# A graph layer on one core: more rows through ACT's DMA queue, and the aggregation with the gathered rows as the stationary side

## The chip, the core and the metric

The kernel runs on one core of one Trainium2 chip. A core has five engines that run side by side, each with its own instruction stream, in order: TensorE (PE; its weight loads are listed as PEld), VectorE (DVE), ScalarE (ACT), GpSimd (POOL) and SyncE (SP). They wait for each other on semaphores. SP, ACT and POOL can also issue DMAs; on SP and ACT these are short instructions of the engine's own queue (listed as SPq and ACTq), on POOL a gather is an instruction of about a microsecond. The metric is the device time of one execution in microseconds; less is better. The time before is a median of three runs.

## What is computed

A layer of a graph network over 12,500 nodes with 128 features and 200,000 edges, sorted by destination node:

```python
h = relu(layernorm(x))
Qv, Ku = h @ W_Q.T, h @ W_K.T
score = einsum('md,md->m', Qv[dst], Ku[src]) / sqrt(128) * exp(-edge_weight)
# of each destination's edges keep the 16 best scores, softmax over them -> alpha
agg = segment_sum(alpha[:, None] * (h[src] @ W_msg.T), dst)
out = x + relu(h @ W_self.T + agg)
```

The sum over a node's edges is linear, so the kernel sums the rows `h[src]` with the softmax's weights first and multiplies the sum by `W_msg` afterwards. The division by the softmax's denominator is a factor for each node and may come before or after that product.

## The kernel before

**Preparation.** The normalized rows `h` are written to a table in HBM (`h_tab`). Edge data are turned so that 128 edges, a chunk, lie on the 128 partitions. Fourteen chunks make a group; there are 112 groups. A group's edges reach the nodes that begin in it; one more chunk, the first of the next group, is looked at with it, so 15 chunks a group.

**Rows.** Each edge needs its source node's row of 512 bytes. Most come by POOL's indirect DMA (L183), one instruction for a chunk of 128 rows, into a buffer `hs` that holds a group; there are eight. `let_go` copies the chunk's indices on DVE (L219) and issues its gathers, two chunks at a time. Of some groups, chunk 13 comes through SP's queue and chunk 12 through ACT's instead, one row a DMA (L803), at a fixed rate: `SP_ROWS = 36` and `ACT_ROWS = 24` rows a pass. The table `slow`, made from these rates, tells which chunks these are. Before a row can be asked for, its number must be in a register of the issuing engine: `rows_named` loads up to 16 at once (L791), `rows_asked` issues so many DMAs.

**The main loop.** Its order is written out by hand (`manual_schedule`), one pass a group, and the stages of several groups are interleaved in it. In pass `i`:

- for group `i + 1`, `far_of` (PE L602, ACT L604, four parts) and `to_edges` (ACT L609) make a matrix that tells which edge belongs to which node; `edges_turned`, `away` (PE L625, ACT L627, three parts) and `places` (ACT L631) make two smaller ones, `po` for an edge's slot at its node and `ow` for the node within a window of 40 nodes that the chunk can reach (`WN = 40`, moved by `STEP = 8` nodes from chunk to chunk);
- for group `i`, `q_to_edges` (PE L642, four parts) brings each edge its node's query, and `scores` (DVE L653) multiplies it with the row;
- for group `i - 1`, `slots_by_node` (PE L667, L669) lays the scores out by node and slot, and `node_by_slots` turns them;
- for group `i - 2`, `best` (DVE L683 and on) finds the 16 best, `kept_to_edges` (PE L712) and `on_edges` (DVE) bring the result back to the edges, `exps` (ACT L729) takes exponentials;
- for group `i - 3`, `weights` (DVE L734) writes the weights `alz` by edge and node, and `sums` (PE L744, two halves of 7 and 8 chunks) adds up weighted rows by node. `alz` has a stretch of zeros around each chunk's 40 nodes, so that the 128 columns that are loaded as the stationary side cover all nodes of the group; the rows are the moving side. `sums_out` (ACT L749) divides by the denominator;
- for group `i - 4`, `sums_turned` (PE L752) and `sums_turned_out` (ACT L756) turn the sums; `products` (PE L759, L760) adds `h @ W_self.T` and the sums times `W_msg.T`; for group `i - 5`, `output` (DVE L764) and `store`.

The order on ACT around the change is, in one pass: `far` 0, the copies L756 and L592, `far` 1, three rows, `far` 2, the exponential of `best`, a copy, `far` 3, `to_edges`, seven rows, two copies, `away` 0, `away` 1, five rows, `away` 2, `sums_out`, `exps`, `places`, the loads of the next rows' numbers, nine rows. On PE the first half of `sums` stands ahead of `away` 0, the second half between `away` 1 and `away` 2. In `more`, `let_go` is called for group `i + 4` (chunks 4 to 13) and, at the end of the pass, for group `i + 5` (chunks 0 to 3); a buffer of `hs` is free when the `sums` of the group that had it are done.

Of the kernel before, what the change touches and what calls it, by code (L numbers as in the profile page):

```python
# [10 lines left out]
F32 = mybir.dt.float32  # L11
# [10 lines left out]
SP_ROWS = 36  # L22
ACT_ROWS = 24
PSUM = bass.MemoryType.PSUM

P = 128
# [9 lines left out]
GC = 14  # L36
NJ = GC + 1
# [44 lines left out]
def gnn_layer(  # L82
# [63 lines left out]

    alz = [const.tile([P, NJ * (WW + STEP)], F32, name=f"alz{i}") for i in range(2)]
    sl1 = [const.tile([P, NJ, KM + 1], F32, name=f"sl1{i}") for i in range(2)]
# [30 lines left out]
    def gather(g, j0, j1, index, table=h_tab):  # L179
        if j0 == 0:  # L180
            T[g]["hs"] = rows_pool.tile([P, GC, D], F32, name="hs", bufs=8)
        for j in range(j0, j1):
            nc.gpsimd.indirect_dma_start(  # L183
                out=T[g]["hs"][:, j, :], out_offset=None, in_=table[0:N, :],
                in_offset=bass.IndirectOffsetOnAxis(ap=index(j), axis=0))
# [104 lines left out]
    with tc.tile_pool(name="edges", bufs=1) as ep, ExitStack() as stage:  # L290
# [53 lines left out]

        jj, eq = (alz[0][0:32, NJ * KM * k:NJ * KM * (k + 1)].rearrange("p (j k) -> p j k", k=KM) for k in range(2))
        nc.gpsimd.iota(jj, pattern=[[1, NJ], [0, KM]], base=0, channel_multiplier=0,
# [9 lines left out]
        load_rows(ew_r, ew)  # L356
        nc.gpsimd.memset(alz[1], 0.0)
        nc.vector.memset(ones, 1.0)
# [42 lines left out]
        for j in range(NJ):  # L401
            nc.vector.memset(w0[:, j:j + 1], float(lead(j)))
        nc.vector.memset(alz[0], 0.0)
        for k in range(2):
# [138 lines left out]
    with tc.tile_pool(name="win", bufs=2) as win:  # L543
# [187 lines left out]
        def weights(g):  # L731
            n, kept = chunks[g], T[g]["kept"]
            nc.vector.tensor_tensor(kept[:, 0:n], T[g]["up"][:, 0:n], kept[:, 0:n], op=OP.mult)
            nc.vector.tensor_tensor(alz[g % 2].rearrange("e (j w) -> e j w", w=WW + STEP)[:, 0:n, 0:WN],  # L734
                                    T[g]["ow"][:, 0:n, :], bc(kept[:, 0:n], WN), op=OP.mult)


        def sums(g, part, at=None):
            n = chunks[g]
            if part == 0:  # L740
                T[g]["pa"] = et[:, 384:384 + P] if at is None else at
            half = n // 2
            for j in range(half) if part == 0 else range(half, n):
                nc.tensor.matmul(T[g]["pa"], lhsT=alz[g % 2][:, WW * j + PRE:WW * j + PRE + P],  # L744
                                 rhs=rows_of(g, j), start=(j == 0), stop=(j == n - 1))

        def sums_out(g):
            T[g]["agn"] = win.tile([P, D], F32, name="agn")
            nc.scalar.activation(T[g]["agn"], T[g]["pa"], AF.Copy, scale=T[g]["rden"])  # L749

        def sums_turned(g):
            nc.tensor.transpose(so[:, 2 * P:3 * P], T[g]["agn"], ident)  # L752

        def sums_turned_out(g):
            T[g]["aggT"] = win.tile([P, P], F32, name="aggT")
            nc.scalar.copy(T[g]["aggT"], so[:, 2 * P:3 * P])  # L756

        def products(g):
            nc.tensor.matmul(so[:, 3 * P:4 * P], lhsT=T[g]["hT"], rhs=wselfT, start=True, stop=False)  # L759
            nc.tensor.matmul(so[:, 3 * P:4 * P], lhsT=T[g]["aggT"], rhs=wmsgT, start=False, stop=True)  # L760

# [57 lines left out]
        for i in range(-3, G - 1):  # L819
# [18 lines left out]
            def more(k):  # L838

                if i in (-1, 0, 1):  # L840
                    g = i + 6
                else:
                    g, k = (i + 4, k + 2) if k < 5 else (i + 5, k - 5)
                    if g < 8:
                        return
                if i >= -1 and g < G:
                    let_go(g, k)
# [5 lines left out]
            more(0)  # L853
            at(i - 4, sums_turned)
            at(i + 1, far_of, 0)
            at(i - 4, sums_turned_out)
            at(i + 1, q_out)
            at(i, q_to_edges, 1)
            at(i + 1, far_of, 1)
            rows_asked("ACT", ACT_ROWS // 8)  # L860
            raw(0)
            for b in range(3):
                at(i - 1, slots_by_node, b)
            at(i + 1, far_of, 2)
            more(1)
            at(i - 2, best)
# [10 lines left out]
            at(i + 1, to_edges)  # L877
            rows_asked("ACT", ACT_ROWS * 5 // 16)
            at(i + 2, h_turned_out)
# [41 lines left out]
        def turned(g):  # L921
            sums_turned(g)
            sums_turned_out(g)

        def begun(g):
            sums(g, 0, bank("a", 1)[:, 0:P])

# [255 lines left out]
```

## Time and profile before

| | |
|---|---|
| median of three runs | 3100.45 us (3090.87 to 3109.37) |
| the profiled execution | 3112.28 us, span 3110.5 us |
| busy PE, PEld | 2052.1, 1692.2 us (66%, 54%) |
| busy DVE, ACT | 1264.1, 1041.8 us (41%, 33%) |
| busy POOL | 1457.7 us (47%) |
| mean granted clock of PE | 0.741 |

A row of a timeline reads: start and length in us from the span's start, engine, line, operation, what it writes and reads, how many like it in a row, and in brackets how long the engine was idle before and what ended that. `remote` there means that the semaphore's update can't be put down to an instruction, `issue` that nothing in the profile explains the wait. In a group's row, the numbers behind the bar are busy time and the mean length in ns, then idle time before it. In a table of windows, each row has the window, its length, then busy time and count of PE, PEld, DVE, ACT and POOL, then PE's granted clock, the share of the DMA engines and GB/s. An f32 matmul is recorded as two matmuls and two weight loads.

### The profile page before, as it was taken

The page shows a single profiled execution, that of the slowest core. Times are in us where ns is not written, and L with a number is a line of the kernel's source. Part 1 is how long each engine was busy: PE and PEld are TensorE (multiplying, and loading weights), DVE is VectorE, ACT ScalarE, POOL GpSimd, SP SyncE. Part 2 cuts the span into 40 slices and gives each one's busy share as a digit, 9 for nine tenths or more (in the row PEclk, how much of TensorE's full clock was granted, in tenths as well). Part 3 has the DMA queues.
Part 4 walks back from the last instruction along what each step waited for, and adds up shares of the span by engine and source line. Part 5 has one row for each costly group of instructions (what it writes and reads, how often), then busy time and mean ns, then how long its engine had stood idle before and what let it go on. Part 6 is the DMA issues. An engine that isn't in the chain of part 4 may idle for free. (4 is left out here: it accounts for less than half of the span.)

```text
span 3110.5 us, 55712 instructions
## 1 busy us (share of the span) xinstructions
PE 2052.1 (66%) x13800; PEld 1692.2 (54%) x13801; DVE 1264.1 (41%) x7016; ACT 1041.8 (33%) x2190; POOL 1457.7 (47%) x1529
## 2 busy tenths in 40 slices
PE   0256666666677667676676666776676666667667
PEld 0145555555555555555565555555565555555556
DVE  4453334433344334443433333434434433344346
ACT  4443323333333233333333333333333332333333
POOL 6524444444444444444444445444445444444440
PEclk9867777767777776777777777767767777777779
DMA  8201111111111111111111111111111111111110
GB/s 218 62 24 43 50 43 42 43 39 44 43 42 44 42 44 42 43 42 42 44 44 42 42 43 44 42 40 43 44 44 44 43 42 42 44 43 41 42 40 12
DMA packets 113004, 144.38 MB, mean 46 GB/s; under 512 B 36775, under 2 KB 86567, under 8 KB 111904
## 3 DMA queue, kind: packets, MB, share of 16 engines
q0 software_dynamic: 48512, 99.39, 12.6%
q1 hardware_dynamic: 59038, 40.04, 4.7%
q8 instruction: 109, 1.79, 0.2%
q14 instruction: 225, 1.84, 0.2%
q10 hardware_dynamic: 5120, 1.32, 0.2%
HBM read 126.79 MB, written 14.40 MB: 45 GB/s over the span
## 5 line engine op out<-in xcount | busy, mean ns | idle before, releaser
L183 POOL DMA_INDIRECT hs<-h_tab,ix x1456 | 1394.9, 958 | 1540.6 <-PE e L744 605.4
L744 PEld LDWEIGHTS e<-hs,alz 128*128 128x128 f32 x3142 | 612.1, 296 | 291.9 <-issue 280.5
L744 PE MATMUL e<-hs,alz 128*128 128x128 f32 x3142 | 668.9, 393 | 0.0
L642 PE MATMUL q<-q,to_e 128*128 128x128 f32 x3348 | 589.9, 324 | 44.9 <-issue 42.9
L642 PEld LDWEIGHTS q<-q,to_e 128*128 128x128 f32 x3348 | 545.9, 234 | 121.5 <-issue 87.5
L604 ACT ACTIVATE far<-a,minus 128x512 bf16<-128x512 f32 (+1 forms) x447 | 294.6, 659 | 891.9 <-issue 344.2
L653 DVE SCALAR_TENSOR_TENSOR prod<-hs,dec_all,q 128x128 f32<-128x128 f32 x1623 | 470.2, 342 | 133.6 <-remote 60.1
L602 PE MATMUL a<-rel,ident 112*128 112x512 bf16 (+1 forms) x447 | 211.0, 472 | 426.0 <-issue 264.4
L627 ACT ACTIVATE aw<-a 128x400 bf16<-128x400 f32 x336 | 169.4, 504 | 836.7 <-PE a L625 450.4
L683 DVE TENSOR_SCALAR ell<-slots,e 128x40 f32<-128x40 f32 x112 | 27.9, 249 | 933.6 <-remote 390.2
L625 PE MATMUL a<-minus_at,pdT 32*128 32x400 bf16 x336 | 146.6, 436 | 376.1 <-ACT aw L627 245.4
L669 PE MATMUL e<-opo,sl 128*41 128x40 f32 x3348 | 236.9, 252 | 34.0 <-issue 33.9
L669 PEld LDWEIGHTS e<-opo,sl 128*41 128x41 f32 x3348 | 215.7, 168 | 43.5 <-issue 31.3
L667 PEld LDWEIGHTS <-zrow 1*41 1x41 bf16 x112 | 11.3, 101 | 412.3 <-issue 412.2
L609 ACT ACTIVATE to_e<-far 128x1920 f32<-128x1920 bf16 x112 | 201.3, 1797 | 3.4
L764 DVE SCALAR_TENSOR_TENSOR o<-s,x_t 128x128 f32<-128x128 f32 x112 | 32.6, 291 | 403.2 <-ACT up L729 350.1
L625 PEld LDWEIGHTS <-pdT 32*128 32x128 bf16 x336 | 31.4, 94 | 190.5 <-ACT pdT L618 122.9
L631 ACT ACTIVATE opo<-aw 128x1200 f32<-128x1200 bf16 x112 | 134.7, 1202 | 0.1
L653 DVE DVE_READ_ACCUMULATOR prod<-hs,dec_all,q 128x1 f32 x1623 | 132.0, 81 | 0.0
L219 DVE COPY ix<-idx_all 128x2 int32<-128x2 int32 (+1 forms) x747 | 126.1, 183 | 0.0
L712 PEld LDWEIGHTS <-to_e 128*128 128x128 bf16 x1674 | 68.0, 111 | 94.4 <-DVE km L695 88.0
L712 PE MATMUL x<-km,to_e 128*128 128x43 bf16 x1674 | 76.7, 202 | 58.4 <-DVE km L695 58.3
(197 smaller groups left out, 1868.0 us busy)
## 6 DMA issues: line engine op xcount, KB each, us to landing
lateSP<-h_tab SPq DMA_DIRECT2D x3968, 0.5 KB
lateACT<-h_tab ACTq DMA_DIRECT2D x2560, 0.5 KB
hs<-h_tab,ix POOLq DMA_INDIRECT x1456
h_r<-h_tab SPq DMA_DIRECT2D x112, 64.0 KB
x_t<-in_x_dram SPq DMA_DIRECT2D x108, 64.0 KB
out_dram<-o SPq DMA_DIRECT2D x108, 64.0 KB
xg<-in_x_dram SPq DMA_DIRECT2D x2, 1400.0 KB
h_tab<-xg SPq DMA_DIRECT2D x2, 1400.0 KB
```

Source lines behind the costliest of these rows:

```text
L183: nc.gpsimd.indirect_dma_start(out=T[g]["hs"][:, j, :], out_offset=None, in_=table[0:N, :], in_offset=bass.IndirectOffsetOnAxis(ap=index(j ...
L602: nc.tensor.matmul(pr[:, 0:n1 - n0], lhsT=upper(ident[0:RR, g:g + 1]).to_broadcast([RR, P]), rhs=rel[:, n0:n1], start=True, stop=True)
L604: nc.scalar.activation(T[g]["far"][:, n0:n1], pr[:, 0:n1 - n0], AF.Square, bias=minus)
L609: nc.scalar.activation(T[g]["to_e"][:, 0:n], T[g]["far"][:, 0:n], AF.Relu, bias=1.0, scale=-1.0)
L625: nc.tensor.matmul(pr[:, 0:400], lhsT=T[g]["pdT"], rhs=minus_at.rearrange("k w j s -> k (w j s)")[:, n0:n1], start=True, stop=True)
L627: nc.scalar.activation(T[g]["aw"][:, n0:n1], pr[:, 0:400], AF.Square)
L631: nc.scalar.activation(T[g]["opo"].rearrange("e w j s -> e (w j s)"), T[g]["aw"], AF.Relu, bias=1.0, scale=-1.0)
L642: nc.tensor.matmul(pq[:, (j - j0) * P:(j - j0 + 1) * P], lhsT=T[g]["to_e"][:, j * P:(j + 1) * P], rhs=T[g]["q"], start=True, stop=True)
L653: nc.vector.scalar_tensor_tensor(prod, rows_of(g, j), dec_all[:, c:c + 1], T[g]["pq", b][:, (j % 4) * P:(j % 4 + 1) * P], op0=OP.mult, op1 ...
L669: nc.tensor.matmul(et[0:KM + 1, STEP * j:STEP * j + WN], lhsT=sl1[g % 2][:, j, :], rhs=T[g]["ow"][:, j, :], start=False, stop=(j == n - 1))
L712: nc.tensor.matmul(px[:, j, 0:KM + 3], lhsT=upper(T[g]["to_e"][:, j * P:(j + 1) * P]), rhs=upper(T[g]["km"]), start=True, stop=True)
L744: nc.tensor.matmul(T[g]["pa"], lhsT=alz[g % 2][:, WW * j + PRE:WW * j + PRE + P], rhs=rows_of(g, j), start=(j == 0), stop=(j == n - 1))
```

## The change

It has three parts.

1. `ACT_ROWS` goes from 24 to 40, and the rows are asked for in more places of the pass: three behind each of `far` 0, 1 and 2, seven behind `to_edges`, three behind each `away`, and 15 behind `places`.
2. In `sums` the sides are exchanged: the gathered rows (128 columns) are loaded as the stationary side, and the chunk's weights, now without zeros around them, are the moving side with 40 columns. Each chunk adds into its window of 40 columns of a PSUM area that a matmul of zeros clears first. The sums come out turned, so the transposition goes: `sums_out` copies them, `messages` multiplies by `W_msg.T`, `messages_out` divides by the denominator, and `products` adds that with the identity as the stationary side.
3. `alz` shrinks from 2400 to 600 columns for each of its two buffers, their two memsets go, and `hs` gets a ninth buffer: `more` lets go one group further ahead.

```diff
-ACT_ROWS = 24
+ACT_ROWS = 40
-    alz = [const.tile([P, NJ * (WW + STEP)], F32, name=f"alz{i}") for i in range(2)]
+    alz = [const.tile([P, NJ, WN], F32, name=f"alz{i}") for i in range(2)]
-            T[g]["hs"] = rows_pool.tile([P, GC, D], F32, name="hs", bufs=8)
+            T[g]["hs"] = rows_pool.tile([P, GC, D], F32, name="hs", bufs=9)
-        nc.gpsimd.memset(alz[1], 0.0)
-        nc.vector.memset(alz[0], 0.0)
...
-            nc.vector.tensor_tensor(alz[g % 2].rearrange("e (j w) -> e j w", w=WW + STEP)[:, 0:n, 0:WN],
+            nc.vector.tensor_tensor(alz[g % 2][:, 0:n, :],
                                     T[g]["ow"][:, 0:n, :], bc(kept[:, 0:n], WN), op=OP.mult)
         def sums(g, part, at=None):
             n = chunks[g]
             if part == 0:
-                T[g]["pa"] = et[:, 384:384 + P] if at is None else at
+                T[g]["pa"] = et[:, 304:304 + WW] if at is None else at
+                nc.tensor.matmul(T[g]["pa"], lhsT=zrow[:, 0:P], rhs=zrow, start=True, stop=False)
             half = n // 2
             for j in range(half) if part == 0 else range(half, n):
-                nc.tensor.matmul(T[g]["pa"], lhsT=alz[g % 2][:, WW * j + PRE:WW * j + PRE + P],
-                                 rhs=rows_of(g, j), start=(j == 0), stop=(j == n - 1))
+                nc.tensor.matmul(T[g]["pa"][:, STEP * j:STEP * j + WN], lhsT=rows_of(g, j),
+                                 rhs=alz[g % 2][:, j, :], start=False, stop=(j == n - 1))
         def sums_out(g):
+            T[g]["aggT"] = win.tile([P, P], F32, name="aggT")
+            nc.scalar.copy(T[g]["aggT"], T[g]["pa"][:, PRE:PRE + P])
+
+        def messages(g):
+            nc.tensor.matmul(so[:, 2 * P:3 * P], lhsT=T[g]["aggT"], rhs=wmsgT, start=True, stop=True)
+
+        def messages_out(g):
             T[g]["agn"] = win.tile([P, D], F32, name="agn")
-            nc.scalar.activation(T[g]["agn"], T[g]["pa"], AF.Copy, scale=T[g]["rden"])
-
-        def sums_turned(g):
-            nc.tensor.transpose(so[:, 2 * P:3 * P], T[g]["agn"], ident)
-
-        def sums_turned_out(g):
-            T[g]["aggT"] = win.tile([P, P], F32, name="aggT")
-            nc.scalar.copy(T[g]["aggT"], so[:, 2 * P:3 * P])
+            nc.scalar.activation(T[g]["agn"], so[:, 2 * P:3 * P], AF.Copy, scale=T[g]["rden"])
         def products(g):
             nc.tensor.matmul(so[:, 3 * P:4 * P], lhsT=T[g]["hT"], rhs=wselfT, start=True, stop=False)
-            nc.tensor.matmul(so[:, 3 * P:4 * P], lhsT=T[g]["aggT"], rhs=wmsgT, start=False, stop=True)
+            nc.tensor.matmul(so[:, 3 * P:4 * P], lhsT=ident, rhs=T[g]["agn"], start=False, stop=True)
...
-                if i in (-1, 0, 1):
+                if i in (-1, 0, 1, 2):
                     g = i + 6
                 else:
-                    g, k = (i + 4, k + 2) if k < 5 else (i + 5, k - 5)
-                    if g < 8:
+                    g, k = (i + 5, k + 2) if k < 5 else (i + 6, k - 5)
+                    if g < 9:
                         return
...
-            at(i - 4, sums_turned)
+            at(i - 4, messages)
             at(i + 1, far_of, 0)
-            at(i - 4, sums_turned_out)
+            rows_asked("ACT", 3)
+            at(i - 4, messages_out)
             at(i + 1, far_of, 1)
-            rows_asked("ACT", ACT_ROWS // 8)
+            rows_asked("ACT", 3)
...
             at(i + 1, far_of, 2)
+            rows_asked("ACT", 3)
...
             at(i + 1, to_edges)
-            rows_asked("ACT", ACT_ROWS * 5 // 16)
+            act_names = rows_named("ACT", i + 1)
+            rows_asked("ACT", 7)
...
             at(i + 1, away, 0)
+            rows_asked("ACT", 3)
...
             at(i + 1, away, 1)
-            rows_asked("ACT")
+            rows_asked("ACT", 3)
             at(i - 3, sums, 1)
...
             at(i + 1, away, 2)
+            rows_asked("ACT", 3)
             at(i - 3, sums_out)
...
             at(i + 1, places)
-            for _ in rows_named("ACT", i + 1):
+            for _ in act_names:
                 pass
-            rows_asked("ACT", ACT_ROWS * 3 // 8)
+            rows_asked("ACT", ACT_ROWS - 25)
```

`rows_named` is a generator, so the loads still happen where it is run through, behind `places`.

More of the change, by code (lines that the diff above doesn't have):

```diff
@@ L343, in gnn_layer @@
                        allow_small_or_imprecise_dtypes=True)
-        jj, eq = (alz[0][0:32, NJ * KM * k:NJ * KM * (k + 1)].rearrange("p (j k) -> p j k", k=KM) for k in range(2))
+        jj, eq = (ep.tile([32, NJ, KM], F32, name=f"jk{k}") for k in range(2))
         nc.gpsimd.iota(jj, pattern=[[1, NJ], [0, KM]], base=0, channel_multiplier=0,
@@ L921, in turned @@
         def turned(g):
-            sums_turned(g)
-            sums_turned_out(g)
+            messages(g)
+            messages_out(g)
         def begun(g):
-            sums(g, 0, bank("a", 1)[:, 0:P])
+            sums(g, 0, bank("a", 1)[:, 0:WW])
         def all_slots(g):
```

## The prediction

> **What bounds the kernel now.** I read the page first, then one pass of the main loop in the timeline, engine by engine, then a pass near the end in which POOL has nothing left to gather, and last the busy times of four whole passes.
>
> ```profile
> span 3110.5 us, 55712 instructions
> ...
> L183 POOL DMA_INDIRECT hs<-h_tab,ix x1456 | 1394.9, 958 | 1540.6 <-PE e L744 605.4
> ...
> L744 PE MATMUL e<-hs,alz 128*128 128x128 f32 x3142 | 668.9, 393 | 0.0
> ...
> lateACT<-h_tab ACTq DMA_DIRECT2D x2560, 0.5 KB
> ```
>
> No engine on the page is near full, so a chain of waits sets the pass. I take one from the start of the long ACT operation `places` (L631) at 1505.94 to the next at 1533.37: 27.43 us. POOL's gathers come in two batches. Left out between the first and the second row are six like them, between the third and the fourth four, all 1.25 us apart (0.94 and a gap of 0.30):
>
> ```profile
> 1504.56 0.95 POOL L183 DMA_INDIRECT hs<-h_tab,ix  x1 [7.72 <-PE e L744]
> ...
> 1513.60 0.94 POOL L183 DMA_INDIRECT hs<-h_tab,ix  x1 [0.30 <-issue]
> 1518.66 0.94 POOL L183 DMA_INDIRECT hs<-h_tab,ix  x1 [4.11 <-DVE prod L653]
> ...
> 1524.90 0.94 POOL L183 DMA_INDIRECT hs<-h_tab,ix  x1 [0.30 <-issue]
> 1531.98 0.95 POOL L183 DMA_INDIRECT hs<-h_tab,ix  x1 [6.13 <-PE e L744]
> ```
>
> The same pass on ACT, PE and DVE (rows of the engines' timelines, ACT first):
>
> ```profile
> 1505.19 0.51 ACT L627 ACTIVATE aw<-a 128x400 bf16<-128x400 f32 x1 [3.65 <-PE a L625]
> 1505.59 0.36 ACT L749 ACTIVATE agn<-e,rden 128x128 f32<-128x128 f32 x1
> ...
> 1505.94 1.20 ACT L631 ACTIVATE opo<-aw 128x1200 f32<-128x1200 bf16 x1
> 1507.77 3.27 ACTq L803 DMA_DIRECT2D lateACT<-h_tab  x9
> 1511.09 0.69 ACT L604 ACTIVATE far<-a,minus 128x512 bf16<-128x512 f32 x1 [3.94 <-issue]
> 1511.67 0.26 ACT L756 COPY aggT<-s 128x128 f32<-128x128 f32 x1
> ...
> 1512.30 0.82 ACTq L803 DMA_DIRECT2D lateACT<-h_tab  x3
> ...
> 1518.97 1.80 ACT L609 ACTIVATE to_e<-far 128x1920 f32<-128x1920 bf16 x1
> 1519.03 2.04 ACTq L803 DMA_DIRECT2D lateACT<-h_tab  x7
> 1521.12 0.27 ACT L585 COPY hT<-s 128x128 f32<-128x128 f32 x1 [0.35 <-PE a L615]
> ...
> 1527.38 0.50 ACT L627 ACTIVATE aw<-a 128x400 bf16<-128x400 f32 x1 [5.68 <-remote]
> ...
> 1533.37 1.20 ACT L631 ACTIVATE opo<-aw 128x1200 f32<-128x1200 bf16 x1
> ...
> 1511.83 0.38 PE L602 MATMUL a<-rel,ident 112*128 112x512 bf16 x1 [3.53 <-ACT far L604]
> ...
> 1512.30 2.32 PE L669 MATMUL e<-opo,sl 128*41 128x40 f32 x30
> ...
> 1522.56 0.34 PE L625 MATMUL a<-minus_at,pdT 32*128 32x400 bf16 x1
> ...
> 1527.94 0.49 PE L625 MATMUL a<-minus_at,pdT 32*128 32x400 bf16 x1 [4.17 <-ACT aw L627]
> 1528.36 3.78 PE L744 MATMUL e<-hs,alz 128*128 128x128 f32 x16
> ...
> 1516.26 0.25 DVE L683 TENSOR_SCALAR ell<-slots,e 128x40 f32<-128x40 f32 x1 [8.64 <-PE a L602]
> ```
>
> Two waits look odd. `best` (DVE L683) needs the slots' matmuls (L669), whose records end at 1514.62, but starts at 1516.26: 1.72 after the first batch ended (1514.54). ACT's first `away` (L627) needs a matmul that ends at 1522.90, but starts at 1527.38: 1.54 after the second batch ended (1525.84). Where nothing is gathered, both waits are gone:
>
> ```profile
> 3033.53 1.48 PE L669 MATMUL e<-opo,sl 128*41 128x40 f32 x30
> 3035.05 0.25 DVE L683 TENSOR_SCALAR ell<-slots,e 128x40 f32<-128x40 f32 x1 [6.05 <-PE e L669]
> ...
> 3040.84 0.34 PE L625 MATMUL a<-minus_at,pdT 32*128 32x400 bf16 x1 [0.41 <-ACT pdT L618]
> ...
> 3041.22 0.50 ACT L627 ACTIVATE aw<-a 128x400 bf16<-128x400 f32 x1 [0.43 <-PE a L625]
> ```
>
> There `best` starts 0.04 after the slots and `away` 0.04 after its matmul. So while a batch is in flight, word from PE comes late, whatever the cause. The loop is then: the second half of `sums` ends and frees a rows buffer; eight gathers (1504.56 to 1514.54, 9.98); 1.72 to `best`; 2.40 to the next gather; six gathers (7.18); 1.54 to `away`; 0.98 to the second `sums`; 3.62 until POOL starts again (1531.98). Together 27.42. Whole passes with 14, 13, 12 and no gathers agree; the column before the clock is POOL (its counts take in a neighbour's gather):
>
> ```profile
> 1505.94:1533.37 27.43, 18.35 (x126) 15.33 (x125) 10.67 (x60) 8.71 (x20) 13.53 (x15) 0.75 0.16 43
> 1990.40:2016.69 26.29, 19.21 (x125) 15.70 (x124) 10.44 (x60) 8.70 (x20) 12.66 (x14) 0.69 0.17 42
> 2126.02:2148.84 22.82, 16.39 (x129) 13.38 (x128) 10.54 (x59) 8.60 (x20) 11.18 (x13) 0.84 0.18 45
> 3027.60:3045.30 17.70, 14.06 (x125) 11.96 (x125) 9.95 (x53) 8.67 (x20) 0.00 (x0) 0.90 0.03 10
> ```
>
> A second chain runs beside the first batch: last `away`, `places`, number loads, nine row issues, `far` (1511.09), PE L602 (1511.83), slots until 1514.62. It has 1516.26 - 1514.62 = 1.64 us to spare. PE idles 3.53 in it, but that idle time costs nothing as long as the batch ends later.
>
> **The change, part by part.**
>
> *Rows off POOL.* 128 rows make one gather. At 24 rows a pass from pass 3 on, 20 gathers leave POOL (2560 / 128); at 40, by the same rule (ready pass, column 12, 111 groups), 33. Thirteen fewer. One is worth 1.25 at least, and by the passes above (27.43 - 22.82) / 2 = 2.3 at most; between them I take 1.7: 22 us gained (16 to 30).
>
> *Rows onto ACT.* Issues start 0.07 after the operation ahead of them and hold the next one: to_e ends at 1520.77, the seven issues at 1521.07, and hT starts at 1521.12. Three behind an operation take 0.82.
> - Behind `far` 0, 1 and 2 and the first two `away`: 0.82 against 0.69, then waits that are there already (`far` 2 is followed by a wait for DVE; the second `away` waits for PE L625 and comes 1.08 after the first). `far` 0 holds the two copies behind it by some 0.3, before `far` 1, which has its matmul to wait for. Nothing; without those waits 0.3 each. Behind to_e stay seven.
> - Behind the last `away` three are new, ahead of `sums_out`, the exponentials, `places` and the number loads. The copy started 0.40 after `away`; now 0.07 + 0.82 + 0.03 = 0.92. That is 0.5 more. The copy without the scale is 0.10 shorter (L756 against L749): net 0.4.
> - Number loads take at most 16 at once: 24 rows need two, 40 need three.
>
> ```profile
> L791 ACTq TENSOR_LOAD <-late_b x213: 551/1041/1241, 215.0 to 3045.1; - x107
> ```
>
>   The third holds 16 numbers: 1.0 to 1.24, I take 1.2.
> - Behind the loads come 15 issues for 9. At 3.27 / 9 = 0.36 six more are 2.2; at 0.27 (0.82 / 3) 1.6. I take 2.1.
>
> So `far` comes 0.4 + 1.2 + 2.1 = 3.7 later. The ends: 0.4 + 1.0 + 1.6 = 3.0, and 0.4 + 1.2 + 3.0 = 4.6 if fifteen in a row slow down to 0.42 each, as nine do from 0.29 (2.04 / 7) to 0.36 (an estimate from these two). The whole of PE's far 1 and the slots is behind it, then `best`, all DVE work after it, and the second batch, whose index copies stand behind `best` on DVE. Of the 3.7, 1.64 is to spare. 2.0 a pass remains (1.4 to 3.0), since the batch is over before the slots begin, and word from PE is then prompt. What is late next is ACT itself.
>
> *Aggregation turned round.* PE does as many pairs as before: stationary rows of 128 columns, moving 40 instead of 128. No row has that shape in f32. L669 (41 stationary, 40 moving) is spaced (2.32 - 0.27) / 29 = 0.07; L744 (128, 128) (3.78 - 0.42) / 15 = 0.22. What decides is which side is waited for:
>
> ```profile
> 97.62 0.63 PE L432 MATMUL s<-row,onerow 1*128 1x112 f32 x2
> ...
> L432 PE MATMUL s<-row,onerow x2: 416/416/416, 97.6 to 97.8; 1*128 1x112 f32 x2
> ...
> 8.26 2.85 PE L322 MATMUL q<-ident,src_r 112*128 112x112 f32 x14 [8.26 <-DVE src_r L381]
> ```
>
> With 112 moving columns L432's second record follows 0.63 - 0.42 = 0.21 after its first, as with 128 moving, while transposes (one pass, L322) with the same 112 are (2.85 - 0.39) / 13 = 0.19 apart. So the 128 stationary columns set 0.21, and 40 moving ones change nothing: 0 a pass (down to 16 x (0.07 - 0.22) = -2.4 if the moving side did). By the Trainium skill (TensorE: Matmul & The Clock Gate, LDWEIGHTS) a load costs its columns over 1.2 in ns, 107 for 128; that would make the second half 1.7 instead of 3.78. Here the pair shows 210, twice that.
>
> The zero matmul at the head of `sums` adds a record, 0.2 at most as between two of L744, ahead of the first half; the matmul behind that half (L625 at 1522.56) starts 4.8 before `away` does. Beside that wait it is nothing, without it 20 us in all. `messages` is two records where the transpose was one, another 0.2 at most, on PE that then waits for `far`; without that wait 20 us too. The multiplication L734 writes as many elements. In the preparation two memsets of 2400 columns go, one of them DVE's:
>
> ```profile
> L403 DVE MEMSET alz<- x1: 2058/2058/2058, 78.0 to 78.0; 128x2400 f32 x1
> ```
>
> That is 2 us gained at most, and nothing if DVE is waited for by no one there; I take 2.
>
> *Ninth buffer.* Gathers run one group further ahead, in the same places of the pass, and wait for the same group's `sums` (i + 6 - 9 = i - 3, as i + 5 - 8). Their data isn't waited for today. Nothing.
>
> *SP* keeps its 36 rows a pass.
>
> **Sum**, against the profiled execution's 3112.28 (span 3110.5): some 104 of the 111 passes have full batches, x 2.0 = +208; two or three with rows and no gathers, with no time to spare, +9; gathers -22; memsets -2. That is +193. The median of the runs shown is 3100.45, 12 lower, so 3293.
>
> **Rivals.**
> - *PE's second half of sums shrinks with the moving columns* (9%). For it: nothing but the shape; against it L432. It stands in the loop, so 2.4 a pass go, or 16 x (0.105 - 0.22) = 1.8 if the stationary side sets half of 0.21: 104 x (2.0 - 2.4 or 1.8) - 15 = -57 or +6: 3043 to 3106.
> - *ACT's rows stay hidden, the change only unloads POOL* (7%). Its place is `far` 0: it decides when `far` comes less than 1.64 later. For it: issues run beside operations; against it: only 1.2 of `places` is there for three loads and 15 issues. Then -22: 3078, faster. The Trainium skill (Perfetto Trace Analysis, Optimizing DMA Performance) advises this balancing of descriptor work over engines.
> - *Late word from PE follows the slots, not the batch* (8%): then nothing is to spare, 104 x 3.7 - 15: about 3470. Against it: the pass without gathers.
> - *The turned matmuls count as less PE work and the clock stays low* (inside the main case): `sums` already run at 0.22, so 0.2 to 0.6 a pass at most, 20 to 60 us.
>
> **How the numbers follow.** Main case 72%, 3293; its own range is 104 x 1.4 to 3.0, about 3230 to 3400. 4% are for what I haven't named. 3150 to 3450 is that, wider by 80 and 50 because passes differ in what they have to spare and for the low clock; it leaves out the two faster rivals and the slowest one. Differences under 0.5% are what measurement of this kernel can hardly tell: faster 0.13 (the hidden rows, most of the shrunk sums, a little else), same 0.04, slower 0.83.
>
> **What would show it.** In the timeline after: 15 issues behind `places` and `far` some 8.4 after `places` began instead of 5.15; PE L602's wait grown from 3.5 to about 7; `best` right behind the slots, no longer 1.7 behind the batch; `away` still 1.5 behind the second batch; `sums` records still 0.21 apart at the low clock; 13 fewer gathers. I'd be wrong if `sums` records came at 0.11 or less at that clock, or if `best` kept its distance to the batch.

## The result, and the profile after

The changed kernel takes 3611.45 us (median of four runs, 3600.66 to 3614.74) against 3098.74 of the kernel before: 1.1646 times, 95% interval 1.1603 to 1.1689. (The 3098.74 is the median of four runs; the forecast was worked out from three of them, 3100.45.) The forecast was 3293, with a range of 3150 to 3450; the direction was right, the size 2.7 times too small (+193 forecast, +513 measured). The profiled execution took 3610.95 against 3112.28, +498.7, or 4.6 us for each of the 108 passes or so that the rows reach.

Each ratio is against the kernel before on the same chip at the same time, which took 3099 to 3154 us beside most runs, but only 2187 beside six of them (e11 to e14, e19 and e20, called "the 2187 runs"; four of these ran on chip 9, which at another time gave 3154).

Two rows of the page before that the prediction doesn't show, ACT's `far` and DVE's `best`:

```profile
L604 ACT ACTIVATE far<-a,minus 128x512 bf16<-128x512 f32 (+1 forms) x447 | 294.6, 659 | 891.9 <-issue 344.2
...
L683 DVE TENSOR_SCALAR ell<-slots,e 128x40 f32<-128x40 f32 x112 | 27.9, 249 | 933.6 <-remote 390.2
```

The page after, the rows that answer to these and to those of before:

```profile
span 3609.2 us, 59581 instructions
...
L183 POOL DMA_INDIRECT hs<-h_tab,ix x1443 | 1378.9, 956 | 2000.2 <-DVE prod L651 920.2
...
L602 ACT ACTIVATE far<-a,minus 128x512 bf16<-128x512 f32 (+1 forms) x447 | 295.8, 662 | 1272.9 <-issue 958.4
L743 PE MATMUL e<-alz,hs 128*128 128x40 f32 x3116 | 566.2, 352 | 0.0
...
L681 DVE TENSOR_SCALAR ell<-slots,e 128x40 f32<-128x40 f32 x112 | 27.9, 250 | 1328.7 <-PE e L667 1316.9
```

There are thirteen gathers fewer (1443), as forecast, and POOL idles 460 us more. ACT idles 381 us more before `far`, mostly in time that the profile can't put down to an instruction it waited for (`issue`, 958.4 for 344.2): that is where its row issues are. `best` now waits for the slots' matmuls (L667), 1316.9 us in all, and no longer for the end of the first batch of gathers. Here is a pass of the timeline, from `places` to `places` 32.04 us, with eight and six gathers like the pass of before; ACT, then POOL (first and last of each batch), PE and DVE:

```profile
1751.63 1.20 ACT L629 ACTIVATE opo<-aw 128x1200 f32<-128x1200 bf16 x1
1754.56 7.72 ACTq L802 DMA_DIRECT2D lateACT<-h_tab  x15
1762.33 0.69 ACT L602 ACTIVATE far<-a,minus 128x512 bf16<-128x512 f32 x1 [9.51 <-issue]
...
1777.38 0.50 ACT L625 ACTIVATE aw<-a 128x400 bf16<-128x400 f32 x1 [5.64 <-remote]
...
1782.46 0.50 ACT L625 ACTIVATE aw<-a 128x400 bf16<-128x400 f32 x1 [3.50 <-PE a L623]
...
1783.67 1.19 ACT L629 ACTIVATE opo<-aw 128x1200 f32<-128x1200 bf16 x1
1749.78 0.95 POOL L183 DMA_INDIRECT hs<-h_tab,ix  x1 [5.89 <-PE e L743]
...
1758.54 0.95 POOL L183 DMA_INDIRECT hs<-h_tab,ix  x1 [0.30 <-issue]
1768.59 0.94 POOL L183 DMA_INDIRECT hs<-h_tab,ix  x1 [9.10 <-DVE prod L651]
...
1774.85 0.95 POOL L183 DMA_INDIRECT hs<-h_tab,ix  x1 [0.31 <-issue]
1763.07 0.59 PE L600 MATMUL a<-rel,ident 112*128 112x512 bf16 x1 [6.85 <-ACT far L602]
...
1763.83 2.32 PE L667 MATMUL e<-opo,sl 128*41 128x40 f32 x30
...
1778.35 2.78 PE L743 MATMUL e<-alz,hs 128*128 128x40 f32 x12
1766.19 0.25 DVE L681 TENSOR_SCALAR ell<-slots,e 128x40 f32<-128x40 f32 x1 [12.73 <-PE e L667]
```

Beside the pass that the prediction shows (27.43):

| step of the pass | before | after | forecast | measured |
|---|---|---|---|---|
| last `away` to `places` | 0.75 | 1.21 | +0.4 | +0.46 |
| `places` to the first row issue (number loads) | 1.83 | 2.93 | +1.2 | +1.10 |
| issues, until `far` 0 | 3.32 | 7.77 | +2.1 | **+4.45** |
| `far` 0 to the slots' end | 3.53 | 3.82 | 0 | +0.29 |
| slots' end to `best` | 1.64 | 0.04 | -1.64 | -1.60 |
| `best` to the second batch's end | 9.58 | 9.61 | 0 | +0.03 |
| its end to `away` 0, to `sums`, to the last `away` | 6.78 | 6.66 | 0 | -0.12 |

One row is over twice its forecast: fifteen issues last 7.77, not some 5.4. It is no single pass: in the mean of the 92 passes with 13 or 14 gathers the issues behind `places` last 7.45, against 3.07 in the mean of 96 such passes before. In the timeline of shorter stretches, the first seven and the last four of the fifteen:

```profile
1754.56 2.37 ACTq L802 DMA_DIRECT2D lateACT<-h_tab  x7
...
1761.19 1.09 ACTq L802 DMA_DIRECT2D lateACT<-h_tab  x4
```

Both go some 0.3 apart. The four between them, from the eighth at 1756.94, take 4.25: the ninth, tenth and eleventh come 1.4 apart. The table of windows over the same stretch shows what ended then:

```profile
1749.78:1751.40 1.62, 1.62 (x7) 1.20 (x8) 0.00 (x0) 0.56 (x2) 1.31 (x2) 0.50 0.00 0
1751.40:1757.20 5.80, 4.82 (x22) 4.40 (x22) 1.36 (x5) 1.42 (x3) 4.36 (x5) 0.58 0.30 80
1757.20:1759.48 2.28, 0.00 (x0) 0.00 (x0) 0.00 (x0) 0.00 (x0) 1.89 (x2) 1.00 0.25 59
1759.48:1760.70 1.22, 0.00 (x0) 0.00 (x0) 0.00 (x0) 0.00 (x0) 0.01 (x1) 0.60 0.22 54
1760.70:1761.50 0.80, 0.00 (x0) 0.00 (x0) 0.00 (x0) 0.00 (x0) 0.00 (x0) 0.50 0.00 1
```

Gathered data moves from 1.6 after the first gather began (1749.78) until 1.2 to 1.4 after the last one ended (1759.49). The Trainium skill (Perfetto Trace Analysis, DMA Instruction — SWDGE (GPSIMD)) says that a gather's profiled end is the end of its descriptors' making and not of its data; these rows agree. So issues become slow while gathered data moves, in this pass from the ninth on. A pass without gathers shows the other side: there the same fifteen take 4.78. SP's issues run beside them in both passes, slowly in the first (twelve in 7.61) and 0.32 apart in the second; so two queues side by side aren't the cause by themselves.

```profile
3475.24 4.78 ACTq L802 DMA_DIRECT2D lateACT<-h_tab  x15
...
1755.45 7.61 SPq L802 DMA_DIRECT2D lateSP<-h_tab  x12
...
3475.43 5.16 SPq L802 DMA_DIRECT2D lateSP<-h_tab  x16
```

What lets the first issues through isn't shown. A fixed count of eight isn't it: in the pass shown SP is held already between its first issue and its second (1755.45 and 1756.92), and in other passes ACT's wait begins behind the ninth to the thirteenth.

### The profile page after: what moved, and what is told of

It reads as the page before. It is cut to its first block, busy times and chain, and to the rows that moved or that the text cites. A ratio compares the mean times of both kernels' runs of the same rounds, so it can differ in the third digit from the quotient of the medians.

```text
span 3609.2 us, 59581 instructions
## 1 busy us (share of the span) xinstructions
PE 2179.6 (60%) x14024; PEld 1845.6 (51%) x14025; DVE 1265.6 (35%) x7011; ACT 1061.5 (29%) x2190; POOL 1439.7 (40%) x1515
## 5 line engine op out<-in xcount | busy, mean ns | idle before, releaser
L183 POOL DMA_INDIRECT hs<-h_tab,ix x1443 | 1378.9, 956 | 2000.2 <-DVE prod L651 920.2
L600 PE MATMUL a<-rel,ident 112*128 112x512 bf16 (+1 forms) x447 | 238.0, 532 | 798.2 <-ACT far L602 777.2
L640 PEld LDWEIGHTS q<-q,to_e 128*128 128x128 f32 x3348 | 665.6, 284 | 52.3 <-issue 22.0
L640 PE MATMUL q<-q,to_e 128*128 128x128 f32 x3348 | 683.9, 370 | 0.0
L743 PEld LDWEIGHTS e<-alz,hs 128*128 128x128 f32 x3116 | 533.4, 263 | 273.8 <-issue 190.3
L602 ACT ACTIVATE far<-a,minus 128x512 bf16<-128x512 f32 (+1 forms) x447 | 295.8, 662 | 1272.9 <-issue 958.4
L743 PE MATMUL e<-alz,hs 128*128 128x40 f32 x3116 | 566.2, 352 | 0.0
L681 DVE TENSOR_SCALAR ell<-slots,e 128x40 f32<-128x40 f32 x112 | 27.9, 250 | 1328.7 <-PE e L667 1316.9
L667 PE MATMUL e<-opo,sl 128*41 128x40 f32 x3348 | 255.9, 268 | 0.0
L667 PEld LDWEIGHTS e<-opo,sl 128*41 128x41 f32 x3348 | 239.5, 186 | 15.0
L723 DVE TENSOR_REDUCE kept<-mine 128x15 f32<-128x600 f32 x112 | 86.9, 776 | 15.5 <-DVE mine L721 12.2
L758 PE MATMUL s<-wselfT,hT 128*128 128x128 f32 x224 | 88.7, 500 | 0.5 <-ACT agn L755 0.5
```

The lines of the kernel that those rows point to most:

```text
L183: nc.gpsimd.indirect_dma_start(out=T[g]["hs"][:, j, :], out_offset=None, in_=table[0:N, :], in_offset=bass.IndirectOffsetOnAxis(ap=index(j ...
L600: nc.tensor.matmul(pr[:, 0:n1 - n0], lhsT=upper(ident[0:RR, g:g + 1]).to_broadcast([RR, P]), rhs=rel[:, n0:n1], start=True, stop=True)
L602: nc.scalar.activation(T[g]["far"][:, n0:n1], pr[:, 0:n1 - n0], AF.Square, bias=minus)
L640: nc.tensor.matmul(pq[:, (j - j0) * P:(j - j0 + 1) * P], lhsT=T[g]["to_e"][:, j * P:(j + 1) * P], rhs=T[g]["q"], start=True, stop=True)
L667: nc.tensor.matmul(et[0:KM + 1, STEP * j:STEP * j + WN], lhsT=sl1[g % 2][:, j, :], rhs=T[g]["ow"][:, j, :], start=False, stop=(j == n - 1))
L743: nc.tensor.matmul(T[g]["pa"][:, STEP * j:STEP * j + WN], lhsT=rows_of(g, j), rhs=alz[g % 2][:, j, :], start=False, stop=(j == n - 1))
```

## The experiments

Theory A: all of the loss comes from ACT's issues that wait while gathered data moves. Rival B: a part of it lies in the turned sums or in the gathers' longer lead.

**The change in its two halves.** e1 is the changed kernel with `ACT_ROWS = 24` and the rows in their old places; e2 is the kernel before with the change's rows:

```diff
-ACT_ROWS = 40
+ACT_ROWS = 24    # e1, from the changed kernel; rows_asked as before
-ACT_ROWS = 24
+ACT_ROWS = 40    # e2, from the kernel before; rows_asked as changed
```

> The change without its rows: 24 rows on ACT's queue in their old places, but the aggregation turned round and the ninth buffer with its longer lead. Theory A (all of the loss comes from row issues that stall on ACT while a batch of gathers is in flight): 3080 to 3120, as before; sums still 0.21 to 0.22 apart, far 0 some 4.8 behind places, best 1.7 behind the first batch. Rival B (part of the loss lies in the turned sums or in the longer lead of the gathers): 3150 to 3350, with a first batch, an away or a half of sums that comes later than before. Rival C (the turned sums are shorter, but the rows hide that): under 3070.

> The rows alone: the kernel before with 40 rows on ACT's queue in their new places, the old aggregation and eight buffers. Theory A: 3580 to 3640, the whole loss; the first eight of the fifteen issues behind places 0.3 apart, the others 0.7 to 1.4 apart until the first batch has landed, far 0 some 10.6 behind places. Rival B: 3250 to 3450, the rest of the loss being the aggregation's.

Measured: e1 3261.37 against 3153.94, 1.0327 (1.0295 to 1.0359); e2 3596.88, 1.1412 (1.1378 to 1.1446). A and B each hold in part: the rows make 14 points (hundredths of the time before), but the turned sums with the ninth buffer and its longer lead make 3. e2 was run again, where the kernel before took 3103.72:

> The kernel of e2_rows_alone (the change's rows, old sums). With the kernel before at some 3100: 1.14 again. With it at some 2190, where far 0 has no time to spare, the chain of the prediction counts in full: 0.5 for the three rows ahead of the copy, 1.1 for the third load, 2.0 for six issues, 3.6 a pass and less 13 gathers: 1.17 to 1.19.

Measured: 3551.57, 1.144 (1.1409 to 1.1471). PE's waits for ACT's `far`, before, in e2 and after (us in all, times, longest):

```profile
PE a L602 <- ACT far L604: 161.2, 106, 17.2
```
```profile
PE a L602 <- ACT far L604: 981.2, 106, 12.7
```
```profile
PE a L600 <- ACT far L602: 777.2, 110, 16.9
```

**The 3 points: sums, shape or lead?** e5 is e1 with eight buffers and the old lead. e10 is the kernel before with one `alz` instead of two, nine buffers and the longer lead. e6 is the kernel before with the sides exchanged, but with all 128 columns, zeros included, as the moving side:

```diff
-            T[g]["hs"] = rows_pool.tile([P, GC, D], F32, name="hs", bufs=9)    # e5, from e1
+            T[g]["hs"] = rows_pool.tile([P, GC, D], F32, name="hs", bufs=8)
-                    g, k = (i + 5, k + 2) if k < 5 else (i + 6, k - 5)
+                    g, k = (i + 4, k + 2) if k < 5 else (i + 5, k - 5)
-nc.tensor.matmul(T[g]["pa"], lhsT=alz[g % 2][:, WW * j + PRE:WW * j + PRE + P],   # e6, from before
-                 rhs=rows_of(g, j), start=(j == 0), stop=(j == n - 1))
+nc.tensor.matmul(T[g]["pa"], lhsT=rows_of(g, j),
+                 rhs=alz[g % 2][:, WW * j + PRE:WW * j + PRE + P], start=(j == 0), stop=(j == n - 1))
-                    g, k = (i + 4, k + 2) if k < 5 else (i + 5, k - 5)    # e10, from before; bufs=9, alz[0] alone
+                    g, k = (i + 5, k + 2) if k < 5 else (i + 6, k - 5)
```

> The turned sums alone (moving side 40 columns, 24 rows in their old places, eight buffers, the old lead of the gathers). e1_turned_24rows was 3.3% slower than the kernel before, at a granted clock of 0.648 against 0.741, with the copy pdT 2.8 later in the pass. Theory E (the turned sums keep PE's clock low, PE comes later to the turned edges, and their word then falls behind the second batch): 1.025 to 1.040 times the kernel before, clock 0.63 to 0.67. Rival F (the longer lead of the gathers costs it): within 0.5% of before, clock 0.73 to 0.75.

> Sides exchanged as in the change, but the moving side is the old 128 columns with the zeros around the 40, so that the shape of the matmuls (128 by 128) is that of before; 24 rows, eight buffers, the old lead. Theory E with the moving columns as its cause: clock 0.73 to 0.75 and 0.995 to 1.01 times the kernel before. If the exchange itself (another stationary side, a product more behind the sums) costs it: 1.025 to 1.04 with a clock of 0.65.

> As e9_nearer_old_sums, but with the longer lead of the change, old sums. Theory E: within 0.5% of the kernel before, since the first batch waits for the same half of sums; clock 0.73 to 0.75. Rival F: 1.025 to 1.04 of before.

Measured against 3146.02: e5 1.0322 (1.0305 to 1.0339), e6 1.0012 (1.0001 to 1.0024), e10 1.0017 (1.0007 to 1.0027); e5 was run again against 3103.72:

> The kernel of e5_sums_alone (turned sums, everything else as before). With the kernel before at some 3100: 1.03 again. With it at some 2190, where the second half of sums stands in the loop of every pass: 16 matmuls of it 0.2 apart instead of 0.13, 1.0 a pass, and as much again in PE's other work at the lower clock: 1.05 to 1.10, clock 0.65 to 0.75. If the clock stays high there: 1.00.

Measured: 1.0275 (1.0247 to 1.0302). The lead and the exchange cost 0.3 points at most: the 40 moving columns, with the matmul of zeros that they need ahead of them, make the 3. Clock and `pdT` (the copy on ACT ahead of `away` 0) of e5, e6 and e10:

```profile
core 0: 3252.9 us, clock 0.656
...
L616 ACT CAST pdT<-a 32x128 bf16<-32x128 f32 x112 | 28.5, 254 | 358.4 <-remote 351.2 <-issue 7.3
```
```profile
core 0: 3166.7 us, clock 0.733
...
L618 ACT CAST pdT<-a 32x128 bf16<-32x128 f32 x112 | 28.4, 253 | 205.5 <-remote 201.6 <-issue 2.9
```
```profile
core 0: 3143.7 us, clock 0.743
...
L617 ACT CAST pdT<-a 32x128 bf16<-32x128 f32 x112 | 28.4, 254 | 192.6 <-remote 173.2 <-issue 18.3
```

With 40 columns the clock falls to 0.656, and ACT waits 150 to 180 us more before `pdT` for a word that the profile puts down to no instruction. In e5 `pdT` comes more than 8 us behind `best` in 76 of the 96 passes with 13 or 14 gathers, in e6 in 38 and in e10 in 37 (of 95). These rows fit the following, which no experiment shows by itself: a slower PE reaches the turned edges after the second batch's data has begun to move, and its word then waits for that data. That the clock follows PE's activity is what the Trainium skill says (TensorE: Matmul & The Clock Gate, Part 1); that 40 columns count for less than 128 here, only these clocks show.

**Place or number of the rows?** e3 is the changed kernel with eight of the fifteen issues moved behind the second `away`; e15 (in a 2187 run: e14) is the kernel before with its 24 rows, fifteen of them behind `places`:

```diff
-            rows_asked("ACT", 3)                # e3: behind away 1
+            rows_asked("ACT", 11)
-            rows_asked("ACT", ACT_ROWS - 25)    # e3: behind places
+            rows_asked("ACT", ACT_ROWS - 33)
-            rows_asked("ACT", ACT_ROWS // 8)    # e14, e15: none behind far 1
-            rows_asked("ACT", ACT_ROWS * 3 // 8)
+            rows_asked("ACT", 15)
```

> The changed kernel with as many rows, but only seven behind places; the eight others stand behind the second away, where ACT waits 3.4 us for the second half of sums and nothing is being gathered. Theory A: far 0 comes some 5.5 to 6.3 behind places instead of 10.6, best is again 1.7 behind the first batch or at most 0.5 later, and the time is 3060 to 3150. Rival B: not under 3250. Rival D (a row's issue costs ACT the same wherever it stands): 3550 to 3620.

> The kernel of e14_fifteen_behind_places (24 rows, fifteen of them behind places, two number loads). There, the kernel before took 2187 and no issue or word was late while gathers were in flight: fifteen issues 0.33 apart, far 0 6.8 behind places. If the kernel before takes some 3100 here: theory A has far 0 at 9.0 to 9.6, best right behind the slots and 1.08 to 1.11 of before; without the stall far 0 at 6.8, and 1.00 to 1.02. If the kernel before takes some 2190 again: 1.10, as there.

Measured for e3: 3286.56, 1.0425 (1.0406 to 1.0444). That is above theory A's 3060 to 3150, which left out the turned sums' 3 points; it is 1 point above e1, with forty rows. Its issues, three behind `far` 0 while data moves and eleven behind `away` 1 when nothing does:

```profile
1606.09 2.86 ACTq L802 DMA_DIRECT2D lateACT<-h_tab  x3
...
1624.94 3.34 ACTq L802 DMA_DIRECT2D lateACT<-h_tab  x11
```

Measured for e15: 3433.94, 1.1062 (1.1032 to 1.1093), with no row and no load more than before. Here are the fifteen, `far` 0 10.45 behind `places` in this pass (9.41 in the mean of the 96 with 13 or 14 gathers; 4.87 in the kernel before), and `best`:

```profile
1737.71 1.20 ACT L631 ACTIVATE opo<-aw 128x1200 f32<-128x1200 bf16 x1
1739.55 8.56 ACTq L803 DMA_DIRECT2D lateACT<-h_tab  x15
1748.16 0.69 ACT L604 ACTIVATE far<-a,minus 128x512 bf16<-128x512 f32 x1 [9.25 <-issue]
...
1752.02 0.25 DVE L683 TENSOR_SCALAR ell<-slots,e 128x40 f32<-128x40 f32 x1 [12.74 <-PE e L669]
```

So the place alone costs 10 points. The same kernel as a 2187 run:

> The kernel before with its 24 rows and its number loads, but fifteen rows behind places (seven behind to_edges, two behind the second away, none behind far 1). Theory A: the issues behind places slow down to 0.7 to 1.4 after the eighth, far 0 comes 9.0 to 9.6 behind places instead of 4.9, best right behind the slots, some 2.5 to 3.2 a pass later: 1.08 to 1.11 of the kernel before. If fifteen issues take 0.33 each, as nine do: far 0 at 6.9, 0.3 a pass, 1.00 to 1.02.

Measured: 2410.25 against 2187.44, 1.1011 (1.0978 to 1.1045), but by another way: the issues stay 0.3 apart, and ACT's `away` follows its matmul by 0.04 between two gathers.

```profile
1327.76 4.74 ACTq L803 DMA_DIRECT2D lateACT<-h_tab  x15
...
1341.71 0.34 PE L625 MATMUL a<-minus_at,pdT 32*128 32x400 bf16 x1 [0.52 <-ACT pdT L618]
1342.09 0.50 ACT L627 ACTIVATE aw<-a 128x400 bf16<-128x400 f32 x1 [0.43 <-PE a L625]
1341.29 0.94 POOL L183 DMA_INDIRECT hs<-h_tab,ix  x1 [0.30 <-DVE rden L706]
1342.54 0.94 POOL L183 DMA_INDIRECT hs<-h_tab,ix  x1 [0.30 <-issue]
```

No word is late there, so `far` 0 has no time to spare: in the 2187 runs `best` starts right behind the slots, even in e12 below, whose `far` 0 comes only 2 us behind `places`. Six more issues at 0.33 are 2.0 a pass, and 104 x 2.0 = 208 of the 223 measured; the expectation's 0.3 a pass for that case forgot this. The changed kernel as a 2187 run:

> The changed kernel beside the other runs, to see whether the parts add up: the rows alone were 1.141 and the turned sums alone 1.032 of the kernel before. If they add: 1.165 to 1.18. If the late far of the rows hides the slower PE of the turned sums: 1.14 to 1.15.

Measured: 2773.68, 1.2671 (1.2633 to 1.2709), above both forecasts. The halves could not be added up there, since neither was run beside it.

**Forty rows in quiet places.** e12 and e18 are one kernel: the kernel before with forty rows, spread, and the number loads behind `pdT`; e19 has the loads behind `places` again:

```diff
+            rows_asked("ACT", 5)     # behind far 2; 3 behind far 1, 8 behind to_edges, 4 behind away 0
+            for _ in rows_named("ACT", i + 1):    # e12, e18: behind edges_turned; e19: behind places, as before
+                pass
-            rows_asked("ACT")
+            rows_asked("ACT", 13)    # behind away 1; 7 behind places (e19: 11 and 9)
```

> The kernel of e12_rows_quiet (40 rows spread, number loads behind pdT, old sums). With the kernel before at some 3100: theory A 0.98 to 1.005, far 0 some 4 behind places at most; rival D (issues cost ACT the same wherever they stand) over 1.08. With it at some 2190: 1.05 again, since there ACT never waits long enough in a pass to hide sixteen more issues and a load.

> Forty rows a pass with the old aggregation, but at places where no gathered data is moving: seven behind places, three behind far 1, five behind far 2, eight behind to_edges, four behind the first away, thirteen behind the second; the number loads behind pdT, where ACT waits anyway. Theory A (a row's issue is dear only while gathered data is moving and some eight issues are already under way): far 0 some 4 behind places, and 0.98 to 1.005 of the kernel before, 13 gathers being saved. Rival D (forty rows cost ACT what they cost wherever they stand): over 1.10.

> As e18_rows_quiet_again (40 rows spread, old sums), but the three number loads are again behind places, with nine issues behind them, and eleven behind the second away. There it was 1.034, and in the passes in which word of pdT came late the loads behind it held the first away by some 2.9. Theory A with that reading, and the kernel before at some 3100: far 0 at 5.9 to 6.3, within the time it has to spare; first away some 0.4 behind the second batch's data again; 0.99 to 1.01. If sixteen more issues cost time even where nothing moves: 1.03 again. With the kernel before at some 2190: over 1.05, far 0 late by 1 to 1.5 in every pass.

Measured for e18: 3212.75 against 3103.72, 1.0345 (1.0318 to 1.0372): far from the 1.144 of the same forty rows in the change's places, yet neither the 0.98 to 1.005 of theory A nor the 1.08 and more of rival D. A late `pdT` shows one place of the loss. The number loads, which the timeline doesn't list, stand between it and `away` 0 (the last one starts at 655.0), though the matmul that `away` 0 needs was over at 653.40:

```profile
652.58 0.25 ACT L618 CAST pdT<-a 32x128 bf16<-32x128 f32 x1 [4.40 <-remote]
655.62 0.50 ACT L627 ACTIVATE aw<-a 128x400 bf16<-128x400 f32 x1 [2.78 <-PE q L642]
...
652.89 0.51 PE L625 MATMUL a<-minus_at,pdT 32*128 32x400 bf16 x1 [5.42 <-ACT pdT L618]
```

e19 was to undo that alone, but came out as a 2187 run: 2532.51, 1.1567 (1.1531 to 1.1603). e12, a 2187 run too, took 2299.25, 1.0502 (1.0465 to 1.0539). Between the two, loads behind `places` and two issues more there cost 233. What sixteen more issues cost in quiet places, where words are late, stays open: 1 point (e3 above e1) or 3.5 (e18, with its loads).

**The first batch sooner.** e4 is e1 with the old lead, e9 the kernel before with one `alz`, nine buffers and the old lead; either way a batch need not wait for the second half of `sums`. e13 and e20, one kernel, are e9 with all eight gathers of the first batch let go there, and few rows behind `places`:

```diff
-            T[g]["hs"] = rows_pool.tile([P, GC, D], F32, name="hs", bufs=8)    # e9, from before
+            T[g]["hs"] = rows_pool.tile([P, GC, D], F32, name="hs", bufs=9)
-            more(5)                  # e13, e20, from e9; more(0) and more(1) go
+            more(5)
+            more(6)
-            more(6)                  # at the end of the pass
+            more(7)
+            more(8)
-            rows_asked("ACT", ACT_ROWS * 3 // 8)
+            rows_asked("ACT", 4)     # 3 behind far 1, 4 behind far 2, 7 behind to_edges, 6 behind away 1; loads behind edges_turned
```

> The kernel of e1_turned_24rows (24 rows, turned sums, nine buffers), but the gathers keep the lead of the kernel before, so that the first batch no longer waits for the second half of sums: its first four gathers can go as soon as their indices are copied, 5 and 3 us earlier. If word from PE to ACT and DVE is late whenever gathers are in flight (the prediction's reading of the two odd waits), the first two aways are now held up until these gathers are over, 2 to 4 us each: 3100 to 3400. If it isn't, the first batch ends 2.2 earlier, the slots then bound best, and 1.75 a pass goes: about 2910. If POOL's start is set by something else than the buffer: as e1.

> The kernel before with a ninth buffer and the old lead, so that the first batch need not wait for the second half of sums; the room for it comes from keeping one alz instead of two. e4_gathers_nearer had this with the turned sums and was 0.968 of before. If the turned sums cost 3% by themselves (theory E): 0.93 to 0.95 of before, clock 0.73 to 0.76. If the turned sums cost nothing (rival F): 0.96 to 0.975. One alz costs nothing by either, since weights are written 1.7 after the sums that read the last ones.

> A version made from what the runs showed: e9_nearer_old_sums (0.973), with the index copies of the first batch all behind the second half of sums' wait, so that its eight gathers go in one row, and with the 24 rows and their number loads moved out of the stretch behind places (four there, three behind far 1, four behind far 2, seven behind to_edges, six behind the second away). If the first batch's data and far 0 together set best, as that run's trace has it (data over at 8.1, slots at 8.3, best at 8.7): best at 6.5 to 7.5, 1.2 to 2.2 a pass less: 0.89 to 0.93. If word from PE during the longer batch comes late for the last away and places: 0.96 to 0.99.

> The kernel of e13_gathers_first, 0.924 where the kernel before takes 2187. With the kernel before at some 3100: its first batch starts 5 before places and goes without a gap, data over at 6.3 to 7 instead of 9.7, far 0 at 2 to 3; but far 1, the last away and places then wait for word while that data moves. By the gain of e9_nearer_old_sums (0.973) and one more us in the batch: 0.93 to 0.96. If the late words eat it: 0.97 to 1.0.

Measured: e4 3052.34, 0.9682 (0.965 to 0.9713), between its two forecasts; e9 3057.69, 0.9728 (0.9703 to 0.9752). POOL's wait for the second half of `sums` is nearly gone in e9 (605.4 before):

```profile
POOL hs L183 <- PE e L743: 24.3, 7, 4.1
ACT aw L626 <- remote: 403.3, 74, 9.0
```

But the gain is 2.7 points only, not the 5 to 7 expected if the turned sums cost 3 by themselves: ACT now waits for word for `away` for 403.3 us in all and up to 9.0 at a time (326.3 and 6.0 before). e9, without the turned sums, isn't better than e4, with them. That speaks for their 3 points hanging on when PE meets the second batch's data, and being gone when the batches lie elsewhere; it isn't shown by itself. e13 and e20, both 2187 runs, took 2021.08, 0.9236 (0.9208 to 0.9263), and 2020.55, 0.9233 (0.9205 to 0.9261), against 2187. They beat both kernels; what they take where the kernel before takes 3100 wasn't measured. In e13 POOL's gathers fill 1406.6 of 2018.8 us, and with the gaps of some 0.30 before each of them over 1800.

## Why the prediction was wrong, point by point

- **Where the time goes** was right: 15 issues behind `places`, `far` 0 late, PE behind it, `best` right behind the slots (0.04), `away` still 1.58 behind the second batch, 13 gathers fewer, `sums` 0.21 apart ((2.78 - 0.42) / 11, from the twelve records of L743 above).
- **The step that failed** is "Rows onto ACT", its last term: "At 3.27 / 9 = 0.36 six more are 2.2; at 0.27 (0.82 / 3) 1.6. I take 2.1", with an upper end of 0.42 each. The runs showed 4.45 a pass. The price per issue was taken from nine issues that were nearly all over before the wait begins, and carried on in a straight line; in the pass shown the first eight are 0.3 each and the next ones up to 1.4 while gathered data moves. A row of before that the prediction doesn't use shows it: SP's issues in the same stretch of the pass it quotes, four in 3.54. The missing 2.35 x 104 is 244 of the 318 by which the median was missed.

```profile
1511.00 3.54 SPq L803 DMA_DIRECT2D lateSP<-h_tab  x4
```

- The other terms of that chain were right to 0.1 in the pass shown: 0.46 for 0.4, 1.10 for 1.2, 1.60 for 1.64 to spare.
- **"Aggregation turned round", 0 a pass**, was right in its argument (the matmuls' spacing is the same) and wrong in its sum: alone it costs 84 to 102 us (1.0275 and 1.0322). The low clock stood among the rivals at 20 to 60, priced by `sums` themselves; by the rows of e5 the cost lies elsewhere, in a `pdT` that waits for late word. In the change some 2 points are left of it (1.1646 against 1.141 and 1.144 of the rows alone), an estimated 60 to 70 us, most of the rest of the 318.
- "Late word" was put down to the batch's end; it fits the end of the batch's data better. In the trace before, `away` 0 starts over 1 us behind its matmul in 80 passes, in the median 0.3 behind the last gathered data. That didn't change the sum, but it is the same stretch that holds the issues, and who sees it has a reason to price the added issues by it.
- Ninth buffer and longer lead, 0: right (1.0017 in e10). Hidden rows and shrunk sums, the rivals on the other side: not so. The rival in which word follows the slots and nothing is to spare, about 3470, was the nearest in size and wrong in its mechanism: 1.60 of the 1.64 to spare was used up, as the main case had it. The Trainium skill's advice on balancing, which the prediction names for the hidden rows, stands under DMA Optimizations in Perfetto Trace Analysis and is for a kernel held up by the making of descriptors; POOL, which makes the gathers' here, was busy 47% of the span.

## What to carry to other kernels

Don't price a further instruction of a queue by the mean of those that are there: look at each issue's spacing, and at what other transfers move meanwhile: in the pass shown the first eight kept their pace, the ninth did not. Issue small DMAs where the profile shows no gather's data moving, and the number loads where nothing waits behind them. And when a matmul's shape changes, look at the granted clock and at everything PE does behind it, not at the matmuls alone.

## What the hardware showed that was not expected

- While gathered data moved, row issues took up to 1.4 instead of 0.3, with the DMA engines 22 to 30% busy (the table of windows). The Trainium skill (DMA: Bandwidth & Descriptors, SWDGE vs HWDGE vs iDMA) has the two kinds of queue feed different internal queues of a DMA engine, served in turn; that alone gives no reason for the issues to wait. Nor is it the DMA issues alone that wait: a register move of ACT between two of them, which takes 0.029 elsewhere, took up to 0.690 in the pass at 1754 (first row). In the 2187 runs, with gathers too, neither does (second row, e14; 4.74 for fifteen issues). No register move among the row issues takes over 0.05 in those six traces; in each of the others 300 to 500 of SP's take over 0.5. So the two can be told apart from a trace; what holds the queues up, and why only at some times, stays open.

```profile
L802 ACTq MOVE lateACT<-h_tab x16: 3/29/690, 1754.5 to 1762.3; - x16
```
```profile
L803 ACTq MOVE lateACT<-h_tab x15: 29/29/29, 1327.7 to 1332.2; - x15
```

- Forty moving columns instead of 128 lowered the granted clock from 0.733 (e6) to 0.656 (e5), with one matmul of zeros more a pass.
